# Self-products of 4096 rows on one core: GpSimd's late input loads as 8 KB packets, dealt over other rows

## The chip, the cores and the metric

The kernel runs on one core of a Trainium2 chip. The metric is the device time of one execution in microseconds (us). Before the change it is 1261.78 us, the median of four runs (1261.73 to 1261.81).

## What is computed

The input has 4096 rows of 256 float32 numbers. Each row is multiplied with itself, every number with every other, and the upper triangle (32896 products) is stored as one row of the output.

```python
dot = jnp.einsum('bi,bj->bij', inputs, inputs)
iu, ju = jnp.triu_indices(d)          # d = 256
return dot[:, iu, ju]                 # 4096 x 32896
```

4 MB are read and 539 MB written.

## The kernel before

**Layout.** Each of the 128 partitions has 32 input rows, in 16 *units* of two rows (2 KB). The tile `x` holds all of them. A *pass* (`h`, 0 to 7) works on two units, `2h` and `2h+1`; it has six *pieces* (`p`, 0 to 5): three thirds of the triangle for the first unit, three for the second. A piece's products, for 2 rows on 128 partitions, fill one of two places `o` (some 43 KB a row and partition) and go out as one store of about 11 MB.

**Who does what.** DVE and GpSimd (POOL in the profile) share the products of a piece, except in the first piece of a pass, which is DVE's alone; a helper weighs the two by times of their instructions (`share`, and `HELP` for the second piece). DVE writes `xv` and, in PSUM, `xp`, copies of the unit for both engines. ScalarE helps in the very first pieces only. The sync engine (SP) issues every store (L397) when DVE's last product of the piece is done; DVE starts a new piece when the store of the piece two before has landed (`free`). The loop over passes is written so that an iteration does pieces 2 to 5 of pass `h` and pieces 0 and 1 of pass `h + 1`.

**Input loads.** Units 0 to 5 are loaded at the start by SP (`NEAR`, L428). The others are loaded by GpSimd (`LATE`), between its products, by the function `late`, which it calls ahead of its products of every piece from 2 to 5. A description such as `(8, 2, 5, 1)` is: from unit 8, two parts, five units apart, of one unit each. The first group is issued at pass 1 piece 5: units 8 and 13 (2 KB each a row), then 6, 7 and 9, 10 (two pieces of 4 KB a row), each as two transfers, of partitions 0 to 119 and 120 to 127 (`MOST`, `halves`). The second group, units 11, 12 and 14, 15, is issued at pass 4 piece 2. At pass 2 piece 5 and pass 5 piece 2 GpSimd waits for the semaphores of what was issued (`far`, `marked`) and drains; it releases DVE only later, through its products of that piece.

**Marks.** Ahead of each load `mark` (L318 to L320) issues a small transfer of 5, 2, 7, 3, 6 and 2 rows (`STEPS`), two pieces of 256 bytes a row, into a tile that nobody reads. `units` (L322) makes the access patterns of a load, L340 issues it.

Of the kernel before, what the change touches and what calls it, by code (L numbers as in the profile page):

```python
# [12 lines left out]
P = 128  # L13
# [2 lines left out]
PIECES = 3  # L16
EDGE = 32
NEAR = [(0, 1, 1, 1), (1, 2, 3, 2), (3, 1, 1, 1)]
LATE = [((1, 5), (2, 5), [(8, 2, 5, 1), (6, 2, 3, 2)]), ((4, 2), (5, 2), [(11, 2, 3, 2)])]
HELPED = 1  # L20
HELP = 16.5
MOST = 120
STEPS = (5, 2, 7, 3, 6, 2)
MARK = 64
PLACES = 2
SETS = 5
# [104 lines left out]
def window(ap: bass.AP, free: list) -> bass.AP:  # L131
    return bass.AP(ap.tensor, ap.offset, [list(ap.ap[0]), *free])
# [3 lines left out]
def kernel(  # L136
# [15 lines left out]
    nc = tc.nc  # L152
# [24 lines left out]
    def semaphore(name: str):  # L177
        return ctx.enter_context(nc.semaphore(name))
# [1 line left out]
    free = [semaphore(f"free{k}") for k in range(PLACES)]  # L180
    head, v_done, a_done, go = (semaphore(s) for s in ("head", "v_done", "a_done", "go"))
    loaded = [semaphore(f"loaded{k}") for k in range(len(NEAR))]
    far, marked = semaphore("far"), semaphore("marked")

    def take(engine, sem, value: int):
        engine.wait_ge(sem, value).then_inc(sem, -value)  # L186
# [131 lines left out]
    def mark(lo: int, hi: int):  # L318
        of = window(x_in[lo:hi], [[2 * MARK, 2], [1, MARK]])
        nc.gpsimd.dma_start(marks[lo:hi, :, :MARK], of).then_inc(marked, 16)  # L320

    def units(of_units: tuple, rows: slice) -> tuple:  # L322
        one, parts, step, of_part = of_units
        dims = [[step * each, parts], [1, of_part * each]]
        return tuple(window(ap[rows, one * each :], dims) for ap in (flat, x_in))

    halves = (slice(0, MOST), slice(MOST, P))

    def late(h, p: int):
        steps, count, at = list(STEPS), 0, 0  # L330
        for begun, had, parts in LATE:
            todo = [(part, rows) for part in parts for rows in halves]
            count += len(todo)
            if p == begun[1]:
                with nc.gpsimd.If(h == begun[0]):
                    for part, rows in todo:
                        step = steps.pop(0)
                        mark(at, at + step)
                        at += step
                        nc.gpsimd.dma_start(*units(part, rows)).then_inc(far, 16)  # L340
            else:
                at += sum(steps[: len(todo)])
                del steps[: len(todo)]
            if p == had[1]:
                with nc.gpsimd.If(h == had[0]):
                    nc.gpsimd.wait_ge(far, 16 * count)
                    nc.gpsimd.wait_ge(marked, 16 * count)
                    nc.gpsimd.drain()

    def gpsimd(h, pieces: range, ahead: bool, done: int = 0, turns: int = 0) -> tuple:  # L350
# [6 lines left out]
        for p in [HELPED] if ahead else pieces:  # L357
            place = places[p % PLACES]
            block, lo = helped(p) if ahead else next((block, lo) for _, _, block, _, lo in blocks(p, False))
            turns += not ahead  # L360
            if not ahead:
                late(h, p)
            order = interleave(block)
            waits = schedule(order)
            counted = {*waits.values()}
            number = {k: done + 1 + c for c, k in enumerate(sorted(counted))}
            for k, ((i, j, at, length), m, _) in enumerate(order):
                at -= lo
                ins = nc.gpsimd.tensor_tensor(  # L369
                    place[:, :, at : at + m * length],  # L370
                    window(xv[:, j:], [[d, REPEAT], [1, m], [1, length]]),
                    window(xv[:, i:], [[d, REPEAT], [1, m], [0, length]]),
                    ALU.mult,
                )
                if k == 0 and not ahead:
                    ins._wait_ge(go, turns)
                elif k in waits:
                    ins._wait_ge(g_own, number[waits[k]])
                if k in counted:
                    ins.then_inc(g_own, 1)  # L380
            done += len(counted)
            ins.then_inc(g_done, 1)
# [88 lines left out]
```

## Time and profile before

| what | us |
|---|---|
| median of four runs | 1261.78 |
| profiled execution, whole | 1261.6 |
| its span, first to last instruction | 1259.8 |
| DVE busy | 822.6 |
| POOL busy | 759.0 |
| landing of a store of 10944 KB after its issue, median of 31 | 35.1 |
| landing of GpSimd's six loads after their issue | 21.9 to 63.3 |

The profile is of one execution. A busy time is the time in which the engine itself worked; issuing a DMA or waiting isn't counted. The DMA lines count packets, one for each contiguous piece that a DMA engine moves (sometimes several pieces), and the time that they took as a share of 16 DMA engines. Queue q1 holds what SP issues, q0 what GpSimd issues. In the answer on waits a line names who waited, for whom, the total, the number of waits and the longest.

### The profile page before, as it was taken

The page shows a single profiled execution, that of the slowest core. Times are in us where ns is not written, and L with a number is a line of the kernel's source. Part 1 is how long each engine was busy: PE and PEld are TensorE (multiplying, and loading weights), DVE is VectorE, ACT ScalarE, POOL GpSimd, SP SyncE. Part 2 cuts the span into 40 slices and gives each one's busy share as a digit, 9 for nine tenths or more (in the row PEclk, how much of TensorE's full clock was granted, in tenths as well). Part 3 has the DMA queues.
Part 4 walks back from the last instruction along what each step waited for, and adds up shares of the span by engine and source line. Part 5 has one row for each costly group of instructions (what it writes and reads, how often), then busy time and mean ns, then how long its engine had stood idle before and what let it go on. Part 6 is the DMA issues. An engine that isn't in the chain of part 4 may idle for free. (4 is left out here: it accounts for less than half of the span.)

```text
span 1259.8 us, 2789 instructions
## 1 busy us (share of the span) xinstructions
DVE 822.6 (65%) x1236; ACT 27.1 (2%) x74; POOL 759.0 (60%) x1143
## 2 busy tenths in 40 slices
DVE  8767657666576665766657666576656766567650
ACT  8000000000000000000000000000000000000000
POOL 5666646685466664666556665476645765467650
DMA  9999999999999999999999999999999999999998
GB/s 396 433 442 427 440 428 440 428 438 429 431 431 437 431 438 427 440 428 441 429 431 434 435 432 437 430 439 429 438 429 439 429 436 431 434 435 431 437 431 376
DMA packets 15719, 543.24 MB, mean 431 GB/s; under 512 B 1223, under 2 KB 1248, under 8 KB 3168
## 3 DMA queue, kind: packets, MB, share of 16 engines
q1 hardware_dynamic: 14704, 540.54, 99.3%
q0 software_dynamic: 1008, 2.64, 0.5%
q14 instruction: 7, 0.06, 0.0%
HBM read 4.21 MB, written 538.97 MB: 431 GB/s over the span
## 5 line engine op out<-in xcount | busy, mean ns | idle before, releaser
L274 DVE TENSOR_TENSOR o<-xv,xp 128x504 f32<-128x504 f32 (+59 forms) x1175 | 791.2, 745 | 398.6 <-DMA out_dram<-o 265.6
L369 POOL TENSOR_TENSOR o<-xv 128x64 f32<-128x64 f32 (+61 forms) x1125 | 750.6, 707 | 455.3 <-DVE o L274 455.1
L302 ACT ACTIVATE o<-x 128x198 f32<-128x198 f32 (+34 forms) x72 | 25.5, 448 | 0.7 <-DMA x<-in_r_inputs_dram 0.7
L253 DVE COPY xp<-x 128x512 f32 x15 | 10.3, 685 | 0.0
L235 DVE TENSOR_TENSOR o<-x,xp 128x470 f32<-128x470 f32 (+18 forms) x19 | 9.7, 584 | 0.0
L235 DVE TENSOR_TENSOR o<-x 128x510 f32<-128x510 f32 (+9 forms) x10 | 5.7, 645 | 2.4 <-DMA x<-in_r_inputs_dram 2.4
L251 DVE COPY xv<-x 128x512 f32 x15 | 6.4, 426 | 0.5
L353 POOL MEMSET xv<- 128x1 f32 x1 | 0.1, 98 | 10.2 <-POOLq L186 10.2
L340 POOL DMA_DIRECT2D x<-in_r_inputs_dram x6 | 4.0, 663 | 0.0
L320 POOL DMA_DIRECT2D marks<-in_r_inputs_dram x6 | 3.7, 611 | 0.0
L431 ACT ACT_TABLE_LOAD x1 | 1.3, 1283 | 1.2 <-ACTq L186 1.2
L429 DVE MEMSET edge<- 128x32 f32 x1 | 0.1, 85 | 1.0 <-SPq L175 1.0
L230 DVE COPY xp<-x 128x512 f32<-128x512 f32 x1 | 0.7, 684 | 0.0
L354 POOL COPY xv<-x 128x512 f32<-128x512 f32 x1 | 0.6, 609 | 0.0
L431 ACT ACTIVATE edge<-edge 128x1 f32<-128x1 f32 x1 | 0.3, 294 | 0.0
L458 POOL MEMSET const-float32-0.0<- 128x1 f32 x1 | 0.1, 98 | 0.2 <-issue 0.2
L458 POOL MEMSET const-bfloat16-1.0<- 128x1 bf16 x1 | 0.1, 101 | 0.0
L458 POOL MEMSET const-uint8-127<- 128x1 uint8 x1 | 0.1, 101 | 0.0
L458 POOL MEMSET const-float32-1.0<- 128x1 f32 x1 | 0.1, 98 | 0.0
## 6 DMA issues: line engine op xcount, KB each, us to landing
out_dram<-o SPq DMA_DIRECT2D x31, 10944.0 KB, 35.1
out_dram<-o SPq DMA_DIRECT2D x16, 11008.0 KB, 32.6
out_dram<-o SPq DMA_DIRECT2D x1, 4352.0 KB, 13.9
out_dram<-o SPq DMA_DIRECT2D x1, 2624.0 KB, 9.6
out_dram<-o SPq DMA_DIRECT2D x1, 1984.0 KB, 7.5
x<-in_r_inputs_dram POOLq DMA_DIRECT2D x2, 960.0 KB, 47.0
out_dram<-o SPq DMA_DIRECT2D x1, 1280.0 KB, 5.5
x<-in_r_inputs_dram SPq DMA_DIRECT2D x1, 1024.0 KB, 5.2
```

Source lines behind the costliest of these rows:

```text
L230: nc.vector.tensor_copy(xp, x_of(h, 0)).then_inc(v_own, 1)
L235: ins = nc.vector.tensor_tensor(place[:, :, at - lo : at - lo + length], window(x_of(h, 0)[:, j:], [[d, REPEAT], [1, 1], [1, length]]), wi ...
L251: ins = nc.vector.tensor_copy(xv[:, :each], x_of(h, p // PIECES))
L253: nc.vector.tensor_copy(xp, x_of(h, p // PIECES)).then_inc(v_own, 1)
L274: ins = nc.vector.tensor_tensor(place[:, :, at : at + m * length], window(xv[:, j:], [[d, REPEAT], [1, m], [1, length]]), window(xp[:, i:] ...
L302: nc.scalar.activation(places[p][:, r, at - lo : at - lo + length], xa[:, r * d + j : r * d + j + length], AF.Copy, scale=xa[:, r * d + i ...
L320: nc.gpsimd.dma_start(marks[lo:hi, :, :MARK], of).then_inc(marked, 16)
L340: nc.gpsimd.dma_start(*units(part, rows)).then_inc(far, 16)
L354: nc.gpsimd.tensor_copy(xv[:, :each], x_of(0, 0)).then_inc(g_own, 1)
L369: ins = nc.gpsimd.tensor_tensor(place[:, :, at : at + m * length], window(xv[:, j:], [[d, REPEAT], [1, m], [1, length]]), window(xv[:, i:] ...
L431: nc.scalar.activation(edge[:, :1], edge[:, 1:2], AF.Copy, scale=edge[:, 2:3])
L458: nc = _bacc.Bacc("TRN2", target_bir_lowering=False, num_devices=1)
```

## The change

All ten late units still come from GpSimd, in six transfers and four marks:

- at pass 1 piece 5: a mark of 5 rows, a load of 20 rows, a mark of 6, a load of 45 rows, each of units 6 to 9 and 11 to 14 as two pieces of 8 KB a row;
- at pass 2 piece 2: a mark of 12 rows, a load of 3, a mark of 2, a load of 60, of the same units; together the 128 rows;
- at pass 3 piece 2: units 10 and 15, 2 KB each a row, over 120 and then 8 rows, without marks;
- GpSimd waits for the eight units at pass 2 piece 5, and for the other two, on a semaphore of their own, at pass 3 piece 5. The wait in pass 5 is gone.

```diff
-LATE = [((1, 5), (2, 5), [(8, 2, 5, 1), (6, 2, 3, 2)]), ((4, 2), (5, 2), [(11, 2, 3, 2)])]
+WIDE, ODD = (6, 2, 5, 4), (10, 2, 5, 1)
+LATE = [
+    ((1, 5), WIDE, [((5,), 20), ((6,), 45)]),
+    ((2, 2), WIDE, [((12,), 3), ((2,), 60)]),
+    ((3, 2), ODD, [((), 120), ((), 8)]),
+]
+HAD = [((2, 5), WIDE, 4, 4), ((3, 5), ODD, 2, 0)]
 HELPED = 1
 HELP = 16.5
-MOST = 120
-STEPS = (5, 2, 7, 3, 6, 2)
...
-    far, marked = semaphore("far"), semaphore("marked")
+    far, marked = {u: semaphore(f"far{u[0]}") for u in (WIDE, ODD)}, semaphore("marked")
...
     def late(h, p: int):
...
+        at, rows = 0, {}
+        for (begun, piece), of_units, parts in LATE:
+            with ExitStack() as when:
+                if p == piece:
+                    when.enter_context(nc.gpsimd.If(h == begun))
+                for steps, count in parts:
+                    row = rows.get(of_units, 0)
+                    rows[of_units] = row + count
+                    for step in steps:
+                        if p == piece:
+                            mark(at, at + step)
                         at += step
...
+                    if p == piece:
+                        nc.gpsimd.dma_start(*units(of_units, slice(row, row + count))).then_inc(far[of_units], 16)
+        for (had, piece), of_units, count, count_of_marks in HAD:
+            if p == piece:
+                with nc.gpsimd.If(h == had):
+                    nc.gpsimd.wait_ge(far[of_units], 16 * count)
+                    if count_of_marks:
+                        nc.gpsimd.wait_ge(marked, 16 * count_of_marks)
                     nc.gpsimd.drain()
```

## The prediction

> **What bounds the kernel.** First the page's header and its DMA part: is the time in transfers or in engines?
>
> ```profile
> span 1259.8 us, 2789 instructions
> ...
> DMA packets 15719, 543.24 MB, mean 431 GB/s; under 512 B 1223, under 2 KB 1248, under 8 KB 3168
> ## 3 DMA queue, kind: packets, MB, share of 16 engines
> q1 hardware_dynamic: 14704, 540.54, 99.3%
> q0 software_dynamic: 1008, 2.64, 0.5%
> ```
>
> Stores (q1) and GpSimd's loads (q0) together fill 99.8% of the span of all 16 DMA engines. DVE and POOL are busy for 65% and 60%. Next the waits: is a store ever late?
>
> ```profile
> POOL o L369 <- DVE o L274: 455.1, 46, 12.0
> DVE o L274 <- DMA out_dram<-o: 265.6, 31, 9.8
> ```
>
> POOL and DVE wait for places that stores free, up to 12.0 and 9.8 us a time; the transfers don't wait for them. A store of 10944 KB lands 35.1 us after its issue, while stores follow every 25.8 us (16 packets of 1.614 us on each of 16 DMA engines), so each is queued some 9 us before its turn. Then stretches (us, busy time of DVE, ACT, POOL, clock, DMA share, GB/s): before, in and after the two times when GpSimd loads.
>
> ```profile
> 200.00:257.00 57.00, 40.80 (x57) 0.00 (x0) 38.16 (x50) 1.00 1.00 431
> 257.00:326.00 69.00, 39.32 (x63) 0.00 (x0) 40.22 (x68) 1.00 1.00 431
> ...
> 650.00:695.00 45.00, 26.60 (x46) 0.00 (x0) 24.94 (x52) 1.00 1.01 433
> ...
> 760.00:1160.00 400.00, 264.90 (x391) 0.00 (x0) 242.88 (x358) 1.00 1.00 434
> ```
>
> The share is 1.00 in all. So a load's bytes cost time, wherever they are put, on the DMA engine that carries them, and the end is that of the engine with most work. Averages over 16 engines can't tell which, so I took the trace's single packet records and strung each to the one that starts within a few ns of its end. This gives 16 chains without a gap from 33 us to the end. They end at 1255.46 to 1256.70 us (thirteen), 1256.81, 1257.60 and, last, **1258.08**; their mean is 1256.30. The remaining 1.7 us of the span and the 1.8 us from it to the profiled execution's 1261.6 stay. Its time is 0.18 below the median 1261.78; I add differences to the median.
>
> Two things in the chains matter. *Who carries what*: one load packet goes between two store packets. Number the DMA engines D0 to D15 from the first that the first mark uses. The mark of five rows puts a 512-byte packet on five engines (D0 to D4), the next mark of two rows on the last of these and on a new one (D4, D5), the load of 8 rows on eight others (D6 to D13), the mark of seven on two new ones and the first five. A transfer thus takes as many engines as the largest divisor of its rows up to 16 (120: 15), starting where the last one ended. Each 120-row load leaves out D4, which gets only packets of 4 or 8 bytes. *D4 is the last chain.* Its store packets take on average 7 ns more than the others' 1618 ns, all along (2.4 us from 700 us to the end); and while the 4 KB loads run, 41 to 186 ns more each. In the two loading stretches that excess is 2.7 us above its usual rate (first half of both: next to none).
>
> **The change, part by part.** Durations of one packet, from the records: 4096 bytes 159 ns, 8192 bytes 309 ns (seven instruction fetches of that size inside the span), the next starting 4 ns early: 155 and 305 net.
>
> *Packets.* A row's ten late units go today as five packets of 4096 bytes (two pieces of 2 KB share one), 775 ns; then as two of 8 KB and one of 4096, 765. So 128 rows save 128 x 10 ns over 16 engines: **-0.1 us** on average. Bounds: 0 if the queue cuts 8 KB into 4 KB; nothing worse in the rows, where a packet costs about 8 ns and 0.0368 ns a byte from 2 KB to 44 KB.
>
> The Trainium skill (DMA: Bandwidth & Descriptors, SWDGE vs HWDGE vs iDMA) prefers packets of at most 4096 bytes, as an engine changes queues only between packets; this speaks against 8 KB. The rows above show no price for a long packet, and a store packet would merely wait 305 ns instead of 155, half as often: by the rule a loss of unstated size, by the rows none.
>
> *Who carries it now.* I deal the new rows by the same law: mark 5 to D0-D4; 20 rows over ten, D5-D14, 2 each; mark 6 to D15-D4; 45 rows over fifteen from D5, 3 each, D4 left out; mark 12 to D4-D15; 3 rows to D0-D2; mark 2 to D3, D4; 60 rows over fifteen from D5, 4 each, D4 out. Then 120 rows of units 10 and 15 without a mark: they start at **D4** and leave out D3; 8 rows go to D3-D10. In KB, before and after: D0-D2 160, 160; D3 160, 116; **D4 0, 36**; D5-D10 160 to 180, 180; D11-D14 168 to 180, 176; D15 160, 144. D5-D10 then spend 18 x 305 + 9 x 155 = 6.89 us on loads; the fullest now spend 45 x 155 = 6.98. So the pack ends where it does now, within 0.1 us. The chain that ended at 1257.60 had 40 load packets and three marks and is one of D0-D3: it ends at 1257.5, or at 1255.8 if it is D3.
>
> *D4, which sets the end.* It takes 8 + 1 packets of 4096 bytes more: **+1.40 us**. Against this stands the excess of 2.7 us: it comes only while the others load and D4 doesn't, and its cause isn't in the trace. Bounds: all 2.7 stays away; or nothing is regained and D4 ends 1.4 us later than now, as the third rival works out. I take it as going with the count of the others' load packets, 27 for 45, since that is the row nearest to it: 2.7 x 18/45 = **-1.1**.
>
> The skill has a guess on such engines (same page, Latency and other measured facts): two of sixteen are often slower, perhaps because the rings of GpSimd's descriptors lie behind their port. Here one is slow, 7 ns a packet; if the guess holds, the excess would go with descriptors, of which there are fewer, and no run so far shows it.
>
> *GpSimd's issues.* Twelve DMA issues of 0.57 to 0.77 us become ten: four in the same place as the eight, four at pass 2 piece 2, two at pass 3 piece 2. They stand before the first product of a piece, and the row there shows the cover: after eight issues
>
> ```profile
> 262.04 0.57 POOL L340 DMA_DIRECT2D x<-in_r_inputs_dram  x1
> 268.84 17.77 POOL L369 TENSOR_TENSOR o<-xv 128x328 f32<-128x328 f32 x44 [6.23 <-DVE o L274]
> ```
>
> POOL still waits 6.23 us for DVE; in pass 2 and 3 it waits 9 to 11 us at every piece, against 2.6 and 1.3 us of issues. Cost 0. If this cover were gone, the 9 us by which stores are queued ahead would be the next. SP's queue isn't touched.
>
> *The waits.* At pass 2 piece 5 and pass 3 piece 5 POOL waits for loads issued three pieces (78 us) before; behind it stand its products of that piece, and DVE's last one, and the store. Today's loads landed within 63.3 us of issue behind more packets (51 on an engine in the first group, now some 18 a group), so they will have landed. Cost 0; if one were late, some 10 us of POOL's slack come first.
>
> Sum: +1.40 - 1.1 = **+0.3 us** on D4, 1258.4; nothing else is later. 1261.6 becomes 1261.9, and the median 1261.78 becomes **1262.1**.
>
> **Rivals.**
> 1. *D4 gets all its lost time back.* It ends at 1258.08 + 1.40 - 2.7 = 1256.8, and the chain at 1257.5 (if in D0-D2) or the pack at 1256.8 is last: -0.6 or -1.3 us, 1261.2 or 1260.5. For it: in the first load, of 2 KB pieces, D4's excess stayed at 9 to 27 ns a packet. Against: two groups out of two had the stall.
> 2. *The forecast*, 1261.4 to 1262.4.
> 3. *D4 can't run ahead.* In the records it was 1.2 us behind the median chain at 257 us, and in both groups it caught up until it was 0.2 to 0.5 ahead and then lost just what the others spent on loads. If that is a limit, the early loads bring it to +0.45 by 350 us, and 906 us at 4.3 ns per us put it 3.4 behind at the end: 1256.1 + 3.4 = 1259.5, +1.4 us, 1263.2. Against: other chains stood 0.7 ahead unharmed.
> 4. *The dealing goes wrong* (slower). The change then doesn't do what it says: of 20, 45 and 60 rows one or more is spread from another start or over another count than I read off 120 and 8, and D4 carries a share of the rows, up to 18 x 305 = 5.5 us. 1.40 + 5.5 - 2.7 (no excess if it loads too) = +4.2 us, 1266.0. It decides once over 2.5 us more lie on D4. For: no transfer of such counts is in the trace. Against: marks of 2, 3, 5, 6, 7 rows and loads of 8 and 120 all obey the law.
>
> Perfect balance would end all at 1256.30 - 0.1, a gain of 1.9 us: less than 0.2% (2.5 us), so a visible gain is out, unless the rows are misread.
>
> **Numbers.** A measurement of this kernel can tell about 0.2% from no change. Forecast 0.34, all regained 0.28, no lead 0.25, dealing wrong 0.08, late waits or a starved queue 0.04, faster beyond reach 0.01. Within 0.2%: 0.34 + 0.28 + 0.25 = 0.87; slower 0.12; faster 0.01. The range goes from full regain, 1260.4, to the limit on the lead with half of its own error, 1263.6, and leaves out 0.13.
>
> **What would show it.** Right: 256 packets of 8 KB in q0 (512 of 4 KB if the queue cuts them), DMA share 1.00 in every stretch, the last chain still D4, with nine 4096-byte packets on it near 491 us and its excess near 1.6 us in the loading times. Wrong: gaps in the chains, packets of 8 KB on D4, waits of POOL on x, or another chain last.

## The result, and the profile after

The changed kernel takes **1263.2 us**, the median of 40 runs (1262.63 to 1263.76). The kernel before, in 60 runs beside it, takes 1261.72 (1261.31 to 1262.25). The ratio is 1.0012, 95% interval 1.0008 to 1.0017: within the 0.2% that were called no change, but 1.5 us longer, and the interval leaves out 1. The number is the third rival's (1263.2) and not the forecast's (1262.1), so the question is where the 1.1 us went that the forecast took off.

The page of the changed kernel first, the lines that answer to those of before:

```profile
span 1261.3 us, 2794 instructions
...
DMA packets 15399, 543.24 MB, mean 431 GB/s; under 512 B 1159, under 2 KB 1184, under 8 KB 2592
## 3 DMA queue, kind: packets, MB, share of 16 engines
q1 hardware_dynamic: 14704, 540.54, 99.2%
q0 software_dynamic: 688, 2.64, 0.5%
```

The bytes are the same, and q0 has 320 packets fewer. The single records behind this line hold 256 packets of 8192 bytes, 309 ns each, and 128 of 4096 bytes, 159 ns each (but for two of 164 and 167), as foreseen. The span is 1.5 us longer, so nothing in these sums shows the loss. The waits of the two busy engines:

```profile
POOL o L373 <- DVE o L278: 456.8, 46, 11.5
DVE o L278 <- DMA out_dram<-o: 267.6, 31, 9.9
```

They grew by 1.7 and 2.0 us in total: the engines wait for stores that end later. They cause nothing. POOL's timeline at the second group (start, duration, what; in brackets the idle time ahead and who ended it):

```profile
337.29 0.61 POOL L324 DMA_DIRECT2D marks<-in_r_inputs_dram  x1
337.90 0.57 POOL L345 DMA_DIRECT2D x<-in_r_inputs_dram  x1
338.47 0.57 POOL L324 DMA_DIRECT2D marks<-in_r_inputs_dram  x1
339.04 0.66 POOL L345 DMA_DIRECT2D x<-in_r_inputs_dram  x1
348.81 1.31 POOL L373 TENSOR_TENSOR o<-xv 128x328 f32<-128x328 f32 x2 [9.11 <-DVE o L278]
```

After 2.4 us of issues POOL still waits 9.11 us for DVE, so the issues are covered. The loads (issue to landing, last column):

```profile
x<-in_r_inputs_dram POOLq DMA_DIRECT2D x1, 960.0 KB, 31.3
x<-in_r_inputs_dram POOLq DMA_DIRECT2D x1, 720.0 KB, 30.7
...
x<-in_r_inputs_dram POOLq DMA_DIRECT2D x1, 32.0 KB, 22.2
```

All land within 31.3 us of issue, and the waits stand 78 us behind it. Stretches as before (the columns are those of the prediction):

```profile
200.00:257.00 57.00, 40.80 (x58) 0.00 (x0) 38.21 (x50) 1.00 1.00 431
262.00:290.00 28.00, 19.53 (x38) 0.00 (x0) 17.81 (x44) 1.00 1.02 438
...
337.00:372.00 35.00, 20.86 (x41) 0.00 (x0) 20.50 (x50) 1.00 1.00 427
372.00:490.00 118.00, 77.39 (x106) 0.00 (x0) 71.93 (x91) 1.00 1.00 434
```

The share is 1.00 to 1.02 in every stretch, but the 60-row load runs at 427 GB/s where the same share gives 434 a moment later. A share of busy time can't tell a packet that moves bytes from one that takes longer over the same bytes; the rate beside it can. The end of the trace shows for whom. Each store packet of 44 KB is put in the microsecond in which it starts, and adds 0.10 to the share. The kernel before, then the changed one:

```profile
1255.00:1256.00 1.00, 0.00 (x0) 0.00 (x0) 0.00 (x0) 1.00 0.31 132
1256.00:1257.00 1.00, 0.00 (x0) 0.00 (x0) 0.00 (x0) 1.00 0.11 44
1257.00:1258.00 1.00, 0.00 (x0) 0.00 (x0) 0.00 (x0) 1.00 0.00 0
```

```profile
1255.00:1256.00 1.00, 0.00 (x0) 0.00 (x0) 0.00 (x0) 1.00 0.31 132
1256.00:1257.00 1.00, 0.00 (x0) 0.00 (x0) 0.00 (x0) 1.00 0.21 88
1257.00:1258.00 1.00, 0.00 (x0) 0.00 (x0) 0.00 (x0) 1.00 0.10 44
```

The last store packet, alone on its DMA engine, starts in 1256 to 1257 before and in 1257 to 1258 after. In the chains it is D4's in both: D4 ends at 1258.07 before and at **1259.52** after, 1.45 later; the next ends at 1257.59 and 1257.78, and the pack at about 1256.3 in both. Between D4's end and the kernel's time lie 3.53 us in both, and 3.52 to 3.54 in the profiled executions of the ten kernels below whose last chain is D4.

Where D4 stood, in us against the median of the 16 chains (plus is ahead), worked out from the single packet records:

| at | before | after |
|---|---|---|
| 257 us, ahead of the first group | -1.2 | -1.2 |
| 330 us | +0.4 | +0.75 |
| 370 us, after the 60-row load | +0.2 | +0.70 |
| 525 us, after units 10 and 15 | -0.4 | 0.0 |
| 655 us | -1.1 | -0.6 |
| 700 us, after the second group of before | +0.5 | -0.8 |
| 1250 us | -1.9 | -3.4 |

In both columns D4 drifts back between the loads: from 700 to 1250 us by 2.4 and 2.6 us, that is 4.4 and 4.7 ns per us. An engine is called *spared* by a load that puts no packet of data on it. The first group gains D4 2.0 us (1.6 before). **The 60-row load, which D4 is spared, gains it nothing**, though each of the others spends eight packets of 8 KB there, 2.44 us. D4's store packets beside a usual engine's, in ns, in the order of their start from 350.6 us on:

```text
D4:      1801  1931  1920  1916  1916  1920  1916  1921  1648  1641
another: 1618  309 1618  309 1618  309 1618  309 1618  309 1618  ...
```

D4's packet is stretched: it takes some 300 ns more, so that it lasts as long as the others' load packet and store packet together. The first line adds up to 2.35 us over 1618 ns a packet, the eight load packets of the second to 2.44. Over the whole way from 241 to 1236 us D4's store packets took 7.3 us before and 7.5 us after more than those of a usual engine (1618 ns, or 1627 for the packets of 44032 bytes), and its load packets none and 1.4.

### The profile page after: what moved, and what is told of

It is laid out like the page before. It is cut to its first block, busy times and chain, and to the rows that moved or that the text cites. A ratio compares the mean times of both kernels' runs of the same rounds, so it can differ in the third digit from the quotient of the medians.

```text
span 1261.3 us, 2794 instructions
## 1 busy us (share of the span) xinstructions
DVE 822.6 (65%) x1236; ACT 27.1 (2%) x74; POOL 758.8 (60%) x1141
## 6 DMA issues: line engine op xcount, KB each, us to landing
x<-in_r_inputs_dram POOLq DMA_DIRECT2D x1, 960.0 KB, 31.3
```

## The experiments

In each, the kernel before ran beside it on the same chip; its median there is given where it isn't 1261.72. "D4" keeps its meaning. The lines of a diff that move GpSimd's waits with the loads are left out and marked by `...`.

**1 and 2. More packets for D4, early or late.** The kernel before, with other marks:

```diff
-STEPS = (5, 2, 7, 3, 6, 2)
+STEPS = (13, 10, 15, 11, 6, 2)
```

with which D4 carries 24 packets of 4096 bytes more from 270 us on, or

```diff
-STEPS = (5, 2, 7, 3, 6, 2)
+STEPS = (5, 2, 7, 3, 14, 10)
```

with which it carries 16 more from 655 us on.

> The kernel before, with other marks in its first group (13, 10, 15, 11 rows), so that the two 120-row loads there leave out D12 and D4 carries 8 + 16 packets of 4096 bytes like the rest. Theory (a DMA engine that is spared gains only until it stands with the first of those that load; what counts is how long D4 then falls behind at 4.3 ns per us): D4 stays 1.2 us behind through the first group, is 2.6 behind at 650 us, and the second group's spare of 2.5 us is then all used: about 2.3 behind at the end, +0.4 us, 1262.2. Rival (each packet put on D4 costs its 155 ns, whenever): 24 x 0.155 = +3.7 us, 1265.4; with the excess of the first group (1.8 us) regained, 1263.6.

> The kernel before, with other marks in its second group only (14 and 10 rows), so that its 120-row load at 650 us leaves out D12 and D4 carries 16 packets of 4096 bytes. Theory: D4 is 1.05 us behind at 650 us, stays so through the load (but for 0.3 of the 8-row load), and falls 2.6 more by the end: 3.4 behind, +1.5 us, 1263.3. That is more than putting 24 packets on it early (1262.2). Rival (packets count, whenever): 16 x 0.155 = +2.5 us, 1264.2, less than the early 24.

Early: 1262.70 us (1262.57 to 1263.05), ratio 1.0008 (0.9999 to 1.0017), +1.0, where the theory had +0.4 and the rival +1.9 or +3.7. Late: 1263.37 (1263.22 to 1263.45), 1.0013 (1.0004 to 1.0022), +1.65, as the theory had it. Twenty-four packets are 3.7 us of work, sixteen 2.5 us; D4's end moves by 1.1 and 1.7. So work on D4 costs less than it lasts, and **the smaller load costs more when it comes later**. In these kernels another engine, D12, is spared in D4's place. It isn't slow in its store packets, yet it gains a little and then its store packets are stretched by some 150 ns each (3 in the first load and 14 in the second; late, 130 ns from the sixth on). The stretch is thus not D4's own.

**3. A mark ahead of units 10 and 15.** The changed kernel:

```diff
-    ((3, 2), ODD, [((), 120), ((), 8)]),
+    ((3, 2), ODD, [((1,), 120), ((2,), 8)]),
...
```

> The changed kernel with marks of 1 and 2 rows ahead of the two loads of units 10 and 15, so that D4 is spared there (0 KB in place of 36) and D3 takes its share. Theory: D4 stood 0.26 us ahead of the median chain before that group; spared 1.4 us it gains until some 0.7 ahead, that is 0.7 more than it has now after the group (0.0): 1262.5. Rival (the 36 KB are the cause): -1.4 us, 1261.8.

1263.06 us (1262.95 to 1263.39), 1.0011 (1.0002 to 1.002): a miss of the edit. A mark of one row put 256 bytes on each of two engines and left the start where it was, so the 120 rows spared D3 again and D4 still carried its eight packets. It tells one thing: D3, about 1 us behind the median, had seven store packets in a row stretched by 86 to 167 ns. An engine need not be at the front to be held.

**4. 8 KB packets on D4.** The changed kernel, the 60-row load begun elsewhere:

```diff
-    ((2, 2), WIDE, [((12,), 3), ((2,), 60)]),
-    ((3, 2), ODD, [((), 120), ((), 8)]),
+    ((2, 2), WIDE, [((12,), 3), ((10,), 60)]),
+    ((3, 2), ODD, [((8,), 120), ((), 8)]),
...
```

> The changed kernel with a mark of 10 rows in place of 2 ahead of the 60-row load, so that it leaves out D12 and D4 carries 8 packets of 8 KB; a mark of 8 rows keeps the third group as it is. Theory: D4 is 0.7 us ahead when that load begins and gains nothing from being spared, so 8 packets more cost nothing: 1263.2, within 0.3. Rival (packets count): 8 x 0.305 = +2.4 us, 1265.6.

1263.79 us (1263.66 to 1264.74), 1.0018 (1.0009 to 1.0027), +0.6 against the changed kernel: outside the 0.3 that the theory allowed, and far from the rival's +2.4. Eight packets of 8 KB, 2.44 us, cost D4 a quarter of what they last; so three quarters of what the sparing was worth by count was never there. D12, spared instead, ran free for three packets, took 103 ns more for the next and then 297 to 309 ns more for each.

**5 and 6. Units 10 and 15 spare D4.** The changed kernel with marks that put the start right, at the old place and a pass later:

```diff
-    ((3, 2), ODD, [((), 120), ((), 8)]),
+    ((3, 2), ODD, [((2, 15), 120), ((2,), 8)]),
...
```

The later form has `(4, 2)` in the place of `(3, 2)`.

> The changed kernel with marks of 2 and 15 rows ahead of the 120-row load of units 10 and 15 and one of 2 ahead of the 8 rows (the single-row mark of the run before left the start where it was, so that D3 was spared again): D4 now really carries 0 KB in place of 36 KB, at 491 us. Theory (a spared engine gains in the first waves of a load only, then its store packets stretch by what the others spend): D4, 0.26 ahead of the median then, gains 0.5 to 0.9 of the 1.24 us and loses nothing to packets of its own (0.25 now): 1262.1 to 1262.5. Rival (packets count): -1.4 us, 1261.8.

> The same, with that group at pass 4 piece 2 (650 us) and its wait at pass 4 piece 5; D4 carries 0 KB. Theory: D4 is then 0.45 us behind and gains nearly all of the 1.24 us, to 0.6 ahead; the 575 us that remain put it 2.0 behind the median at the end (3.4 now): 1261.8. Rival (packets count, whenever): the same time as the run in which the group stands at 491 us.

At the old place 1262.91 us (1261.94 to 1263.75), 1.0008 (0.9999 to 1.0017); a pass later 1262.34 (1261.63 to 1263.39), 1.0004 (0.9995 to 1.0013); before 1261.93. The median of the later form is lower by 0.57, where the theory has 0.67 (155 us at 4.3 ns) and the rival nothing. But these two kernels vary by 1.8 us from run to run, the kernel before by 0.9 at most, so eleven runs of each don't tell 0.57 from nothing; and the levels are 0.4 to 0.8 above what was expected. The one profiled execution of the later form is the longest, 1263.39: there D4 gained only 0.9 us in the first group, in place of 2.0. What a sparing brings is not the same in each execution.

**7. The source of the wide loads.** The changed kernel, its wide loads read from other units of `x` in SBUF (so units 6 to 9 and 11 to 14 hold copies of units 0 to 3 and 1 to 4, not their input):

```diff
+        if of_units == WIDE:
+            return window(flat[rows, one * each :], dims), window(flat[rows, :], [[each, parts], dims[1]])
```

> The changed kernel with the loads of the eight units taken from x itself (units 0 to 4) in place of HBM: same rows, packets, engines and places in time, so later passes compute products of wrong rows. If the stretch of a spared engine's store packets comes from the others' reads of HBM, it goes, D4 gains 3.0 us in the first group and 2.4 in the second and is no longer last: 1261.5 or less, by the chain of D0 to D2 that ends next. If it comes from the writes into SBUF, from the packets without data, or from how descriptors are dealt, the 300 ns a packet stay: 1263.2.

1268.53 us (1267.61 to 1269.51), 1.0052 (1.0038 to 1.0065), before 1261.93. In the two stretches of the wide loads

```profile
262.00:290.00 28.00, 19.53 (x38) 0.00 (x0) 17.77 (x44) 1.00 1.01 388
337.00:372.00 35.00, 23.37 (x42) 0.00 (x0) 24.20 (x50) 1.00 1.00 411
```

the share is 1.01 and 1.00 as with HBM as the source, and the rate 388 and 411 GB/s against 438 and 427. Packets grew on most engines, load packets of 309 ns up to 1973 and store packets of 1618 ns up to 3844. So store packets can be stretched though the loads don't read HBM, but with so much slower the run can't tell what stretches a spared engine. Inconclusive for its question.

**8 and 9. Small groups, spread over the passes.** If a spared engine gains only in the first packets of a group, many small groups should bring more. Five groups of two units, one piece of 4 KB a row; then four groups of two pieces a row, over 112 and 16 rows:

```diff
+U = [(6, 1, 1, 2), (8, 1, 1, 2), (10, 1, 1, 2), (12, 1, 1, 2), (14, 1, 1, 2)]
+MARKS = [(5, 2), (7, 3), (5, 3), (7, 3), (6, 3)]
+LATE = [((2 + k, 2), u, [((m,), 120), ((n,), 8)]) for k, (u, (m, n)) in enumerate(zip(U, MARKS))]
...
```

```diff
+U = [(6, 2, 3, 2), (8, 2, 3, 1), (12, 2, 2, 1), (13, 2, 2, 1)]
+LATE = [
+    ((1, 5), U[0], [((5,), 112), ((), 16)]),
+    ((3, 2), U[1], [((2,), 112), ((), 16)]),
+    ((5, 2), U[2], [((2,), 112), ((), 16)]),
+    ((5, 5), U[3], [((2,), 112), ((), 16)]),
+]
...
```

> The changed kernel with its loads in five groups: at piece 2 of passes 2 to 6 the two units of the next pass (one piece of 4 KB a row, 120 and 8 rows, each with a mark); four of the 120-row loads spare D4, the third spares D3; the waits stand at piece 5 of the same pass. Theory: D4 falls 0.7 us behind from one group to the next and gains 0.5 to 0.9 in each that spares it, so it is near the others until 970 us and some 1.0 behind at the end (1.9 in the kernel before): 1260.8. Rival (packets count): D4 is spared 4 x 9 packets, 0.6 us fewer than the 40 of the kernel before: 1262.3.

> The changed kernel with its loads in four groups, each in two pieces a row so that the dealing law holds: units 6, 7, 9, 10 at pass 1 piece 5; 8, 11 at pass 3 piece 2; 12, 14 at pass 5 piece 2; 13, 15 at pass 5 piece 5. Each is a mark (5 rows, then 2), a load of 112 rows, which 14 engines carry, so that D3 and D4 are both spared, and one of 16 rows over all 16. Theory: D4 gains about 1 us in each group and falls 1 to 1.3 us between them, so it stands near the median at 890 us and 1.2 to 1.6 behind at the end (1.9 in the kernel before, 3.4 in the changed one); D3, 2.1 behind at 257 us, gains at least 0.7: 1260.9 to 1261.4. Rival (packets count, whenever): D4 carries 5 packets, the kernel before none: 1262.5.

Both missed, by how the rows were dealt. Five groups: 1266.22 us (1266.15 to 1266.4), 1.0034 (1.0022 to 1.0046), before 1261.93. Rows of a single piece don't follow the law of rows of two: the 120 rows left out the same other engine each time, whatever the marks, and the 8 rows went to the same eight, D4 among them. D4 carried nine packets a group and ended 5.7 us behind the median. Also, from 1074 us on its lateness reached the stores:

```profile
1074.00:1076.00 2.00, 0.91 (x2) 0.00 (x0) 0.00 (x0) 1.00 0.93 396
```

A share of 0.93, as eleven of the other engines had no packet for some 0.3 to 0.7 us: a store lands only when D4 has done its part, DVE gets the place later, and the next store is late for all (this one was issued at 1074.3 us, 1070.0 in the kernel before). D4's own chain has no gap there, so its end, and with it the time, is still its own work.

Four groups: 1265.03 us (1264.96 to 1265.23), 1.0027 (1.0017 to 1.0037), before 1261.74. Here the law held and the count was wrong: 16 divides 112, so all sixteen engines carried 7 rows, and the 16 rows one each. Every engine got 40 packets, D4 too, and no store packet was stretched, as none was spared. D4 ended 5.69 us behind. **Equal shares cost 3.3 us** (1265.03 - 1261.74), the value of sparing D4 as the kernel before does it. Eight of the other engines had no packet for 0.2 to 0.3 us near 1152 us; D4's chain has no gap there either.

**10. No late loads at all.** The changed kernel without its late loads, marks and waits; units 6 to 15 are zeros:

```diff
-            if not ahead:
-                late(h, p)
...
+    nc.gpsimd.memset(xt[:, 3:, :], 0.0)
+    nc.gpsimd.drain()
```

> The changed kernel without any of GpSimd's loads, marks and waits for them; units 6 to 15 are zeros that GpSimd writes at the start, so later products are zeros. All loads together are 6.9 us on a usual DMA engine. If D4's 7 ns a store packet have nothing to do with the loads, it falls 5.2 us behind the others by the end, which themselves end 6.9 us earlier: 1261.7 + 5.2 - 1.9 - 6.9 = 1258.1. If the loads cause D4's slowness, all engines end nearly together: about 1255, by the chain with the instruction fetches.

1258.44 us (1258.34 to 1258.59), 0.9974 (0.9964 to 0.9984), before 1261.74. From its page:

```profile
DMA packets 14711, 540.60 MB, mean 430 GB/s; under 512 B 880, under 2 KB 880, under 8 KB 2160
...
q1 hardware_dynamic: 14704, 540.54, 99.5%
q14 instruction: 7, 0.06, 0.0%
```

There is no q0 at all. The end of its trace, in stretches of one microsecond as above:

```profile
1249.00:1250.00 1.00, 0.00 (x0) 0.00 (x0) 0.00 (x0) 1.00 0.11 44
1250.00:1251.00 1.00, 0.00 (x0) 0.00 (x0) 0.00 (x0) 1.00 0.10 44
...
1253.00:1254.00 1.00, 0.00 (x0) 0.00 (x0) 0.00 (x0) 1.00 0.10 44
```

From 1249 us on one store packet starts at a time, where the two kernels of the result give 0.4 to 1.4 until 1255 us. With no packet of GpSimd in the trace, D4 drifts as before: from -1.0 us at 257 to -5.6 at 1240, 4.7 ns per us. The pack ends near 1249.3, two more chains at 1250.38 and 1251.27, and D4 goes on alone until 1254.89. The time is 0.3 above the 1258.1 that was expected if D4's slowness has nothing to do with the loads, and 3.4 above the other value. So the drift has nothing to do with GpSimd's DMAs. All ten late units cost 3.3 us (1261.74 - 1258.44) in the kernel before and 4.8 in the changed one, though they are 6.9 us of packets on a usual engine: in the kernel before the others load in time that D4 needs for its stores anyway.

The Trainium skill (DMA: Bandwidth & Descriptors, Latency and other measured facts) guesses at the rings of GpSimd's descriptors behind the slow engines. Here one engine is as slow without any such descriptor, so for this kernel the measurement speaks against the guess.

**11 and 12. The last sparing later.** Four groups as in 9, but 120 and 8 rows with marks that spare D4 each time; and the kernel before with only its second group issued 78 us later:

```diff
+    ((1, 5), U[0], [((5,), 120), ((2,), 8)]),
+    ((3, 2), U[1], [((7,), 120), ((3,), 8)]),
+    ((5, 2), U[2], [((6,), 120), ((2,), 8)]),
+    ((5, 5), U[3], [((7,), 120), ((3,), 8)]),
...
```

```diff
-LATE = [((1, 5), (2, 5), [(8, 2, 5, 1), (6, 2, 3, 2)]), ((4, 2), (5, 2), [(11, 2, 3, 2)])]
+LATE = [((1, 5), (2, 5), [(8, 2, 5, 1), (6, 2, 3, 2)]), ((4, 5), (5, 2), [(11, 2, 3, 2)])]
```

> All ten late units in four groups (passes 1, 3, 5 and 5), 120 and 8 rows each, with marks that put the start of each 120-row load so that D4 is the one left out every time; bytes per DMA engine as in the kernel before. Theory (each sparing sets D4 back to about the front, and what counts is the time from the last one to the end, here some 410 us shorter than in the kernel before, at 4.3 ns per us, less what it lost by being spared of shorter packets there): D4 ends 0.2 to 0.6 us ahead of what it did, behind the next chain by little, 1261.0 to 1261.5 us. Rival (only the count of packets matters, and D4's has not changed): 1261.7 us, with D4 last by 0.5 us as before.

> The kernel before with its second group issued three pieces later (pass 4 piece 5, 78 us later); bytes and dealing unchanged. Theory (D4 is set back to the front at the last sparing and then loses 4.3 ns per us): 78 x 4.3 ns = 0.3 us less, 1261.4 us, and D4 1.6 in place of 1.9 us behind at 1250 us. Rival (when a load runs does not matter): 1261.7 us.

Four groups: **1261.28 us** (1261.08 to 1261.5, 11 runs), before 1261.97 (1261.8 to 1262.6, 21 runs); ratio 0.9994 (0.9985 to 1.0003). Second group later: 1261.64 (1261.37 to 1262.12, 11 runs), 0.9998 (0.9989 to 1.0007). The medians move by -0.69 and -0.33, as the theory said (-0.2 to -0.7 and -0.3), but both intervals take in 1, so neither is shown to beat the kernel before (with four groups the slowest run is below the fastest of the kernel before; the other form's runs overlap it). The chains, of one execution each, fit the theory. With the group moved, D4 was 1.5 us behind at 1250 us and not 1.9, and ended at 1257.84 and not 1258.07. With four groups D4 stood at the median (0.0) at 930 us, after the last one, and ended at 1257.87; there another chain, 2.35 behind ahead of the first group and 1.5 behind at the end, was the last, at 1258.09. So D4 no longer set the end in that execution.

## Why the prediction was right or wrong

- **What bounds the kernel**: right. In every kernel here the last chain of packets plus 3.4 to 3.5 us is the time. Some chains have idle time in 7, 8, 9 and 10, 0.8 us at most in one place, but not those that ended last.
- **Packets** (-0.1): right in kind: 256 of 8192 bytes at 309 ns, so they aren't cut and a long packet has no price of its own. On the pack's end, 1256.3 in both, 0.1 us doesn't show.
- **Who carries it now**: right for all six loads, D4 with nine packets of 4096 bytes, D3 spared in the third group. Rival 4 is out.
- **D4's nine packets** (+1.40): right. D4's end moved by 1.45.
- **The excess regained** (-1.1): **the step that failed.** "I take it as going with the count of the others' load packets, 27 for 45." The excess in the loading stretches came to some 3.1 us by the records (0.7 in the 45-row load, 2.35 in the 60-row load), where the step had 1.6 and the kernel before 2.7. Where it comes, it goes with the *time* of the others' load packets: 300 ns for an 8 KB packet, 150 for one of 4 KB. It came after three free packets for D12 in 4, after five for D12 in the late load of 2, and from the first on for D4 in the 60-row load and for D3 in 3. Halving the number of packets at twice the length regains nothing. The measured term is about 0: D4's store packets cost 7.3 us over a usual engine's before and 7.5 after, and the end moved by 1.45 where the nine packets alone make 1.40.
- **Rival 3**, with a chance of 0.25, had the number (1263.2, D4 3.4 behind; measured 1263.2, 3.4) and its working: early sparings end in a lead of +0.7 (it said +0.45), and then the drift runs for 900 us. That the number fits to a tenth is luck: the lead was 0.25 us larger than it said, and the drift 4.7 ns per us and not 4.3. That a sparing brings less than it takes off the engine is shown by 1, 2 and 4; that the time from the last sparing to the end counts is borne out by 1 and 2, fits the single chains of 11 and 12, and is not told by 6. Its reason, a limit on D4's lead, isn't: other engines were held as well, D12 when 0.9 to 1.2 us ahead (1, 2 and 4), but D3 while about 1 us behind the median (3, and the third group of the changed kernel, where D3 gained 0.15 of 1.2).
- **GpSimd's issues and waits** (0): right, POOL still waits 8.5 to 10 us for DVE after them, and no load is waited for.
- **The range**: it held the time because the price of "no lead" was in it, not because the forecast's own sum held.

What stays **open** is what stretches the store packets of an engine that isn't given load packets. It isn't slow store packets of its own (D12), nor a place at the front (D3); whether it is the loads' reads from HBM (7 couldn't tell), their writes to SBUF, the empty packets of 4 or 8 bytes that the spared engine gets, or how stores and loads take turns among the engines was not told apart. Why an engine is held from a load's first packet on in one case and later in another is open too. That the gain of one sparing differs between executions (6) is open as well.

## What to carry to other kernels

When transfers bound a kernel, string the packet records of each DMA engine into a chain and look at which ends last; the average share, here 1.00 all along, hides it. An engine that is spared gained only at the start of a load here, if at all, and a change that joins groups early lost what the later one gave. Sparing a slow engine in several short groups, the last of them late, is what this points to; run 11 fits it, but no run shows it clear of noise. Before counting on a dealing of rows, read from the records who got them: two pieces a row, one piece a row and a single row were dealt by different rules here.

## What the runs showed of the hardware that was not expected

- One of the 16 DMA engines takes some 7 ns more for each store packet of 1618 ns, 4.3 to 4.7 ns per us, with or without GpSimd's loads (10), on both chips that the experiments ran on.
- A spared engine's store packets take 1.74 to 1.78 us beside 4 KB loads and 1.92 us beside 8 KB loads, in place of 1.62 to 1.63, once the engine is held (after none to five packets of a load).
- A load on few engines costs these more than its packets: with 3 rows on D0 to D2, the store packet ahead took 515 to 591 ns more, on top of two packets of 309 ns.
- Rows of two pieces: as many engines as the largest divisor of the rows up to 16, from where the last transfer ended (112 rows: all 16; 120: 15). Rows of one piece: 120 rows as 8 each on the same 15 engines, 8 rows on the same 8, and the start doesn't move. The Trainium skill (DMA: Bandwidth & Descriptors, Why a DMA increments its semaphore by 16 and not by 1) has both: the divisor with a moving start, and, as an exception for some of GpSimd's copies, rows over 16 rounded up for each engine, which gives these 8. Runs 8 and 9 agree; which copies are the exception it doesn't say.
